# Attention with a conditioned query and key on one core: step 29 keeps its exponentials, six loads change their queue, two first blocks are loaded as halves

## The chip, the core and the metric

The kernel runs on one core of a Trainium2 chip. A core has five engines that run beside each other, each with its own queue of instructions in a fixed order: TensorE (PE in the profile; PEld is its loading of weights) for matrix products, VectorE (DVE), ScalarE (ACT), GpSimd (POOL) and SyncE (SP), which here only issues DMAs. ScalarE and GpSimd issue DMAs too. An engine that waits for a semaphore holds everything behind it in its queue. PE writes its results to PSUM, eight banks of 128 partitions by 512 floats; VectorE and ScalarE read them there.

The metric is the time of one execution in microseconds on the device. Lower is better.

## What is computed

`x` is (8, 512, 512), `cond` (8, 512), the three weights (512, 512), all float32. There are 16 heads of 32 columns.

```python
Q = split_heads(x @ Wq.T + bq);  K = split_heads(x @ Wk.T + bk);  V = split_heads(x @ Wv.T + bv)
cQ = Q + split_heads(tokens @ Wq.T + bq)     # tokens = cond[:, None, :]
cK = K + split_heads(tokens @ Wk.T + bk)
scores = einsum('bhqd,bhkd->bhqk', cQ, cK) / sqrt(32)
out = einsum('bhqk,bhkd->bhqd', softmax(scores), V)
return x + merge_heads(out)
```

## The kernel before

**Steps.** The 8 batches and 16 heads are worked in 32 steps: step `t` is batch `t // 4` and a group `t % 4` of four heads, which fill the 128 partitions, 32 columns each. All matrices lie in SBUF; q and k of a step are held turned (`qkT`), V as rows (`vs`). The products of x with the weights are made in pairs of steps, seven quarter products in place of eight (`product`, line 451), and are spread as three items over each step of the loop (`MADE`, line 1090).

**Two ways to the exponentials.** For each step the scores are computed twice. In the *row pass* (`row_max`, line 593, and `row_scores`, 639) queries lie on the partitions: VectorE takes the row maxima, and ScalarE (`denominators`, 678) takes exponentials with the maxima as bias and adds them up, which gives the denominators. In the *crossed pass* keys lie on the partitions: the maxima, turned and split in three bfloat16 parts, are put into PSUM by a small product with ones, and the scores are added on top, so that ScalarE takes plain exponentials (`exponentials`, 742). These are multiplied by V (`times_v`, 791).

**Kept steps.** For the steps in `KEPT` (line 71), steps 1 to 28, the exponentials of the first half of the queries (`qc < KQ`, two of four blocks) are kept from the row pass in `store` (`kept[t]`, `room`). They are turned in place: VectorE turns 32x32 blocks (`turn_kept`, 656; four instructions of 128x1024 for a step), and DMAs swap the blocks across partitions (`swap_kept`, 665) in three moves of six DMAs each: aside, across, and back. The first and last move are issued by GpSimd for the most part, the rest by SyncE. Only the other half of the queries is computed crosswise (`exponentials_of_rest`, 762: two calls for a step, each of which covers two of the four key blocks), and the product with V is made by halves (`times_v_half`, 802). Step 29, 30 and 31 are not kept: `exponentials` or `crossed` (1270) computes all of their exponentials, four calls for a step.

**The loop** `thirds(t)` (1133) does, for `t` from 1 to 28: row passes of step `t + 1`, the rest of the exponentials of `t`, the weighted sum of `t - 1` with its store (`weighted`, `send`), three items of products, and the turning and swapping of step `t + 1`'s kept half.

**The order is written out by hand** for PE, ScalarE, VectorE and GpSimd (`manual_schedule`, line 235): each runs its instructions in the order of the program text. SyncE's DMAs are ordered by a scheduler, by the program text where they are ready. DMAs from SyncE and ScalarE share eight semaphores in turn, so each waits until the DMA eight places before it has landed. `TURNS`, `begin` and `released` say which PSUM banks each stage uses.

**The start** (lines 245 to 1013). Wq's first block, x's first and second block and Wk's first block are loaded, then the condition and the biases, the rest of x's first batch and of Wq (lines 245 to 264). Then SyncE issues, at line 270, sixteen loads of Wk and sixteen of Wv, each a 32-row slice in turned order, so that VectorE can finish the turn (`turn_w`, 963). PE runs products with ones while it waits (line 925), then turns blocks of Wq and x and makes the first projections. `condition` (900) multiplies the condition by the turned weights, `condition_end` (908) turns that and adds the bias, and `project_qk_end` (412) adds it to q or k. With q and k of step 0 at hand, `row_max(0, 0)` (line 988) begins the steady work. `transpose_x` (350), for the third and fourth block of x, also queues the loads of the next batch's blocks (line 363, `load_block`).

**The end** (lines 1309 to 1431). Steps 29 to 31 have no products left. `crossed` mixes the row pass of one step with the crossed pass of another; `part_of` (1023) makes a step's product with V in pieces and adds the pieces on GpSimd; `send_parts` divides and stores. For steps 30 and 31 the denominators are sums of the exponentials (`sum_of`, 1256) multiplied by ones (`times_ones`, 818). Step 31 ends with the lines 1398 to 1430; line 1431 issues the last quarter of step 30's store.

Of the kernel before, what the change touches and what calls it, by code (L numbers as in the profile page):

```python
# [17 lines left out]
def kernel(  # L18
# [38 lines left out]
    nc = tc.nc  # L57
# [13 lines left out]
    KEPT = range(1, T - 3)  # L71
# [173 lines left out]
    load_w("q", Wq, nc.sync, [0])  # L245
    load_x(0, nc.scalar)
# [19 lines left out]
    for n, w, f in (("k", Wk, HG), ("v", Wv, 0)):  # L266
        wn = ws[n].rearrange("p c (f e) -> p c f e", e=BL)
        for cc in range(NC):
            for h in range(HG):
                nc.sync.dma_start(  # L270
                    wn[h * BL : (h + 1) * BL, cc, f:], spread(w, cc * P + h * BL)[:, f:]
                )
    bvl = const.tile([P, 1], F32, tag="bvl", name="bvl")
    nc.sync.dma_start(bvl, bv.rearrange("(g p o) -> g p o", g=G, o=1)[G - 1])
    bvs = const.tile([P, G, BL], F32, tag="bvs", name="bvs")
    for h in range(HG):
        nc.sync.dma_start(
            bvs[h * BL : (h + 1) * BL],
            bv.rearrange("(o g h e) -> o h g e", o=1, g=G, h=HG)[:, h].broadcast_to([BL, G, BL]),
        )  # L280


# [382 lines left out]
    def swap_kept(t, move, last=nc.gpsimd):  # L665

        later = 6 if t % 4 == 1 else 1
# [4 lines left out]
        for n, (a, g) in enumerate(APART):  # L672
# [3 lines left out]
            (last if move == 2 or move == 0 and n >= later else nc.sync).dma_start(to, of)  # L676
# [248 lines left out]
    for _ in range(28):  # L925
        nc.tensor.matmul(warm[:, :P], onesb, onesb, start=True, stop=True)
# [26 lines left out]
    transpose_x(3, bank(3), nc.scalar.copy)  # L953
    first_part("k", pk, 0)
# [63 lines left out]
    parted = []  # L1018

# [3 lines left out]
    def part_of(t, pt, of, between=None):  # L1023

        if t in KEPT:
            for half in (1, 0):
                for kc in of:
                    times_v_half(t, kc, half, pt, of)
        else:
            for k, kc in enumerate(of):  # L1030
                if k and between:
                    between()
                times_v(t, kc, pt, of)
        if t in parts:
            p = late_part(3 + len(parted))
            parted.append(t)
            nc.scalar.copy(p, pt)
            nc.gpsimd.tensor_tensor(parts[t], parts[t], p, ALU.add)
        else:
            if not parts:  # L1040
# [422 lines left out]
```

## Time and profile before

| | |
|---|---|
| median of 3 runs | 656.83 us (656.81 to 657.03) |
| profiled execution | 658.96 us |
| its span, first to last instruction | 657.0 us |
| granted TensorE clock | 1.000 |
| DMA queue of SyncE | 232068 packets, 61.08 MB, 49.3% of 16 engines' span |
| DMA queue of GpSimd | 13104 packets, 35.80 MB, 20.4% |
| DMA queue of ScalarE | 1760 packets, 1.05 MB, 0.5% |

How to read the lines that follow in this document. A timeline row is: start, duration (both us from the start of the span), engine, line, operation, what it writes and reads, shape, number of instructions that were merged, and in brackets the idle time before it with what ended it. SPq, ACTq and POOLq rows are issues of DMAs. PE's float32 products show as two records each, and four products on 32 partitions run beside each other. A row of the chain of waits is start, duration, engine, tile and line. A row of a table by stage is the stretch, its length, and for each engine the busy time and in brackets the number of instructions, then PE's clock, the busy share of the DMA engines, and GB/s.

### The profile page before, as it was taken

To read this page: it belongs to the slowest core of one execution; us is meant where nothing else is said; L and a number is where in the kernel's file an instruction comes from. 1 tells how busy PE (TensorE), PEld (TensorE's weight loads), DVE (VectorE), ACT (ScalarE), POOL (GpSimd) and SP (SyncE) were. 2 spreads that over 40 slices of the span, in tenths; PEclk is the share of its full clock that TensorE was granted. 3 is DMA by queue.
4 is the path that set the end of the run, shared out by engine and by line. 5 is a ranking of instruction groups with operands and counts; after the bars stand their busy time and mean duration, and the time that the engine had idled before them with its cause. 6 is when DMAs were issued, how large, how long until landed. Compare 5 with 4: busy or idle time off the path is not lost.

```text
span 657.0 us, 24808 instructions
## 1 busy us (share of the span) xinstructions
PE 649.0 (99%) x9836; PEld 349.7 (53%) x9836; DVE 591.8 (90%) x823; ACT 539.4 (82%) x1372; POOL 442.8 (67%) x702
## 2 busy tenths in 40 slices
PE   9999999999999999999999999999999999999997
PEld 8345455555555555555555555555555555555432
DVE  3699999999999999999988999999999999897777
ACT  2479888889888888988887988888898888898774
POOL 3542566886767776578767777678677777767461
PEclk9999999999999999999999999999999999999999
DMA  6634587878777788878897877787889767687111
GB/s 181 105 51 66 125 167 162 174 171 187 177 158 161 150 181 180 178 160 172 187 174 162 187 159 168 169 188 162 180 192 169 158 138 165 155 176 167 27 35 32
DMA packets 247048, 99.51 MB, mean 151 GB/s; under 512 B 229130, under 2 KB 229642, under 8 KB 246932
## 3 DMA queue, kind: packets, MB, share of 16 engines
q1 hardware_dynamic: 232068, 61.08, 49.3%
q0 software_dynamic: 13104, 35.80, 20.4%
q8 instruction: 77, 1.26, 0.9%
q10 hardware_dynamic: 1760, 1.05, 0.5%
q14 instruction: 39, 0.32, 0.2%
HBM read 19.75 MB, written 8.39 MB: 43 GB/s over the span
## 4 chain that ended last, share of the span: by engine, by line
PE 92%; DMA 3%; SPq 2%; DVE 1%; issue 1%; ACT 0%; POOL 0%; DVEq 0%; ACTq 0%; POOLq 0%
PE psum L461 42%; PE psum L641 18%; PE psum L810 15%; PE psum L779 7%; PE psum L768 3%; PE psum L794 2%; DMA store<-store 2%; SPq L270 1%; PE psum L750 1%; PE psum L404 1%; DMA store<-in_L_cond_Wk_dram 1%; PE psum L1287 1%; PE psum L820 1%; PE psum L747 0%; DVE nmax L650 0%
## 5 line engine op out<-in xcount | busy, mean ns | idle before, releaser
L695 ACT ACTIVATE psum<-psum,nmax 128x512 f32<-128x512 f32 x255 | 169.4, 669 | 4.8 <-DVE nmax L589 3.9
L676 POOL DMA_DIRECT2D store<-store x273 | 136.1, 503 | 42.0 <-DMA store<-store 27.1
L695 ACT ACTIVATE store<-psum,nmax 128x512 f32<-128x512 f32 x197 | 135.3, 701 | 34.7 <-DVE nmax L589 25.3
L589 DVE TENSOR_REDUCE nmax<-psum 128x1 f32<-128x512 f32 x220 | 141.3, 679 | 20.5 <-PE psum L641 18.3
L650 DVE TENSOR_REDUCE nmax<-psum 128x2 f32<-128x1024 f32 x126 | 152.7, 1213 | 1.3 <-PE psum L641 1.3
L641 PE MATMUL psum<-kT,qT 32*128 32x512 f32 x1024 | 145.1, 616 | 0.0
L789 ACT ACTIVATE store<-psum 128x512 f32<-128x512 f32 x224 | 115.7, 602 | 23.4 <-PE psum L779 23.4
L660 DVE STREAM_TRANSPOSE store<-store 128x1024 f32<-128x1024 f32 x112 | 134.2, 1218 | 0.0
L810 PE MATMUL psum<-store,v 128*32 128x256 f32 x1792 | 103.1, 381 | 1.3 <-issue 1.3
L810 PEld LDWEIGHTS psum<-store,v 128*32 128x32 f32 x1792 | 55.2, 110 | 57.5 <-ACT wT_q L628 20.5
L641 PEld LDWEIGHTS psum<-kT,qT 32*128 32x128 f32 x1024 | 56.6, 183 | 35.9 <-issue 21.1
L883 POOL TENSOR_TENSOR res<-res,recs 128x512 f32<-128x512 f32 x30 | 31.4, 1047 | 60.2 <-DVE res L882 60.0
L779 PE MATMUL psum<-qT,kT 32*128 32x256 f32 x896 | 57.9, 373 | 0.0
L695 ACT ACTIVATION_READ_ACCUMULATOR psum<-psum,nmax 128x1 f32 x255 | 54.2, 213 | 0.0
L461 PE MATMUL psum<-wc_v,xc 128*32 128x256 f32 x768 | 47.7, 379 | 0.0
L204 POOL TENSOR_TENSOR xr<-xr,bvs 128x512 f32<-128x512 f32 x30 | 38.5, 1282 | 11.2 <-DMA x<-in_x_dram 11.1
L779 PEld LDWEIGHTS psum<-qT,kT 32*128 32x128 f32 x896 | 43.9, 184 | 3.5
L461 PE MATMUL psum<-xc,wc_q 128*32 128x256 f32 x720 | 44.6, 379 | 0.0
L461 PE MATMUL psum<-xc,wc_k 128*32 128x256 f32 x720 | 44.5, 379 | 0.0
L695 ACT ACTIVATION_READ_ACCUMULATOR store<-psum,nmax 128x1 f32 x197 | 42.5, 216 | 0.0
L884 POOL TENSOR_TENSOR res<-res,xr 128x512 f32<-128x512 f32 x30 | 38.4, 1279 | 2.4
L461 PE MATMUL psum<-xT,wT_k 128*32 128x256 f32 x480 | 34.5, 382 | 0.0
(193 smaller groups left out, 1027.1 us busy)
## 6 DMA issues: line engine op xcount, KB each, us to landing
store<-store POOLq DMA_DIRECT2D x273, 128.0 KB, 3.6
store<-store SPq DMA_DIRECT2D x231, 128.0 KB, 2.4
out_dram<-res SPq DMA_DIRECT2D x122, 64.0 KB, 3.4
xr<-in_x_dram SPq DMA_DIRECT2D x120, 64.0 KB, 2.7
x<-in_x_dram SPq DMA_DIRECT2D x112, 64.0 KB, 3.0
w_q<-in_L_cond_Wq_dram SPq DMA_DIRECT2D x4, 256.0 KB, 4.1
w_v<-in_L_cond_Wv_dram SPq DMA_DIRECT2D x16, 64.0 KB, 2.5
w_k<-in_L_cond_Wk_dram SPq DMA_DIRECT2D x16, 48.0 KB, 2.9
```

The costliest lines, as they stand in the source:

```text
L204: nc.gpsimd.tensor_tensor(xr[t], xr[t], bias, ALU.add)
L461: nc.tensor.matmul(pt[r], still[:, r], moving, start=(kc == kcs[0]), stop=(kc == kcs[-1]))
L589: nc.vector.tensor_reduce(nmax[t][:, qc, j : j + 1, 0], pt, AX.X, ALU.max, negate=True)
L641: nc.tensor.matmul(pt, qkT["q", t][r, qc * P : (qc + 1) * P], qkT["k", t][r, :], start=True, stop=True,)
L650: nc.vector.tensor_reduce(nmax[t][:, qc, pr * 2 : pr * 2 + 2, 0], pt, AX.X, ALU.max, negate=True)
L660: nc.vector.transpose(e, e)
L676: (last if move == 2 or move == 0 and n >= later else nc.sync).dma_start(to, of)
L695: nc.scalar.activation(to, of, AF.Exp, bias=nmax[t][:, qc, j, :], accum_out=sums[t][:, qc, j, :],)
L779: nc.tensor.matmul(bank[j][:, i * HS : (i + 1) * HS], qkT["k", t][r, kc * P : (kc + 1) * P], qkT["q", t][r, rest], start=False, stop=(i == 1),
L789: nc.scalar.activation(e[:, i, :], bank[pr * 2 + i], AF.Exp)
L810: nc.tensor.matmul(pt[j * HD : (j + 1) * HD, half * HS : (half + 1) * HS], vs[b % 2][:, kc, (g * HG + j) * HD : (g * HG + j + 1) * HD], e, ...
L884: nc.gpsimd.tensor_tensor(y, y, xr.pop(t), ALU.add)
```

## The change

`KEPT` takes in step 29, so steps 1 to 29 are kept. The loop still runs for steps 1 to 28. In step 28 VectorE turns step 29's kept half, two pieces after the first item and two after the second (`TURNED_LAST`), its maxima are turned by a DMA as in the other steps, and its swaps are issued after the second item, three of the first move and three of the last by SyncE. In the other steps SyncE issues two of the first six moves where it issued one (all six in every fourth step, as before).

Step 29 is written anew: two row passes of step 30, the two halves of step 28's product with V around the first `exponentials_of_rest(29)`, a row pass of step 30, the second `exponentials_of_rest(29)`, half of step 29's product around a row pass of step 31 and the turning of step 30's maxima, which is behind `split_max` on VectorE. The second half of step 29's product follows in step 30. The pieces are no longer added on GpSimd, since each half is complete.

In the last steps GpSimd makes two of the sums of exponentials that VectorE made (`sum_of(t, acc, 2)` and `3`, second pair). ScalarE copies the last denominators out of PSUM and VectorE then multiplies the copy; they are turned ahead of the last block. The last quarter of step 30's store moves from ScalarE's last instruction to SyncE.

At the start the first block of Wq and of x are each loaded as two halves of 64 rows, one from SyncE and one from ScalarE. Of Wk's sixteen loads SyncE issues ten; ScalarE issues six, behind its copy for the fourth block of x. Wv's loads and `bv` stand behind these in the text, so also behind the loads that `transpose_x` queues. Four of 28 products with ones go. `condition("k")` moves straight behind `condition("q")`.

```diff
-    KEPT = range(1, T - 3)
+    KEPT = range(1, T - 2)
...
-    load_w("q", Wq, nc.sync, [0])
-    load_x(0, nc.scalar)
+    xs[0] = early[:, 3, :]
+    for to, of in ((ws["q"][:, 0, :], Wq[:P, :]), (xs[0], x[0, :P, :])):
+        nc.sync.dma_start(to[: P // 2], of[: P // 2])
+        nc.scalar.dma_start(to[P // 2 :], of[P // 2 :])
     load_x(1)
...
-    for n, w, f in (("k", Wk, HG), ("v", Wv, 0)):
+    def load_spread(n, w, f, ccs, queue=nc.sync, hs=range(HG)):
         wn = ws[n].rearrange("p c (f e) -> p c f e", e=BL)
-        for cc in range(NC):
-            for h in range(HG):
-                nc.sync.dma_start(
+        for cc in ccs:
+            for h in hs:
+                queue.dma_start(
                     wn[h * BL : (h + 1) * BL, cc, f:], spread(w, cc * P + h * BL)[:, f:]
                 )
...
+    load_spread("k", Wk, HG, (0, 1))
+    load_spread("k", Wk, HG, (2,), nc.sync, (0, 1))
...
-        later = 6 if t % 4 == 1 else 1
+        later = 3 if t == KEPT[-1] else 6 if t % 4 == 1 else 2
...
-            (last if move == 2 or move == 0 and n >= later else nc.sync).dma_start(to, of)
+            here = n >= later if t == KEPT[-1] else move == 2 or move == 0 and n >= later
+            (last if here and move != 1 else nc.sync).dma_start(to, of)
...
-    for _ in range(28):
+    for _ in range(24):
...
     transpose_x(2, bank(0))
     transpose_x(3, bank(3), nc.scalar.copy)
+    load_spread("k", Wk, HG, (2,), nc.scalar, (2, 3))
+    load_spread("k", Wk, HG, (3,), nc.scalar)
+    load_spread("v", Wv, 0, range(NC))
...
     condition("q", bank(6))
+    condition("k", bank(5))
     project_qk_part(1, "q", 0, bank(7))
     condition_end("q", bank(1), nc.vector)
     project_qk_end(0, "q", pq)
-    condition("k", bank(5))
...
+    TURNED_LAST = {(0, 2): 2, (1, 2): 2}
...
-    for t in KEPT:
+    for t in KEPT[:-1]:
         thirds(t, iter(MADE[(t - 1) % G * 3 :]))
...
     t = T - 3
-    row(4)
-    exponentials(t, 0)
-    row_max(t + 1, 1)
+    begin(0, HG)
+    first, second = row_of[0][:HG], row_of[0][HG:]
+    row_max_aside(t + 1, 1)
+    for j in range(HG):
+        row_scores(t + 1, 2, j, banks(HG + j))
+    for j in range(2):
+        nc.scalar.copy(late_part(j), banks(HG + j))
+    max_aside(t + 1, 1)
...
+    swap_kept(t, 2)
+    halves_of(t - 1, banks(0), (1,))
+    row_of[0] = [*second[:2], *first[2:], *first]
+    exponentials_of_rest(t, 0)
+    halves_of(t - 1, banks(HG), (0,))
...
+    row_max(t + 1, 3, False, HG)
+    split_max(t + 1, nc.vector)
+    exponentials_of_rest(t, 1)
+    row_of[0] = [second[0], first[3], first[1], first[0], first[2], *second[1:]]
+    halves_of(t, banks(0), (1,), (0, 1))
+    row_max(t + 2, 0, False, HG)
+    transpose_max(t + 1, banks(1), nc.scalar.copy)
+    halves_of(t, banks(0), (1,), (2, 3))
...
     t = T - 2
...
-    part_of(t - 1, banks(2), [2, 3])
+    halves_of(t - 1, banks(2), (0,))
...
-    sum_of(t, acc, 1, nc.vector, [0])
-    sum_of(t, acc, 2, nc.vector)
+    sum_of(t, acc, 2, nc.gpsimd, [1])
+    for kc in (1, 2):
+        sum_of(t, acc, kc, nc.vector, [0])
...
-    sum_of(t - 1, acc, 3, nc.vector)
+    sum_of(t - 1, acc, 3, nc.gpsimd, [1])
+    sum_of(t - 1, acc, 3, nc.vector, [0])
...
-    store_30(nc.sync, (0, 1))
+    store_30(nc.sync, (0, 1, 3))
...
-    nc.vector.tensor_tensor(part_x, pd, xr[t], ALU.mult)
...
     nc.scalar.copy(den, pd)
+    nc.vector.tensor_tensor(part_x, den, xr[t], ALU.mult)
...
-    store_30(nc.scalar, (3,))
```

More of the change, by code (lines that the diff above doesn't have):

```diff
@@ L1016, with halves_of, part_of @@
     parts = {}
-    parted = []
     def late_part(i):
         return late[0][:, i, :]
[L1023 to L1040, printed above, removed]
-                parts["all"] = stage.tile([P, NC, D], F32, tag="w", name="parts")
-            parts[t] = parts["all"][:, t % NC, :]
-            nc.scalar.copy(parts[t], pt)
+    def halves_of(t, pt, halves, among=range(NS)):
+        for half in halves:
+            for kc in among:
+                times_v_half(t, kc, half, pt)
+    def part_of(t, pt, of):
+        for kc in of:
+            times_v(t, kc, pt, of)
+        parts[t] = stage.tile([P, NC, D], F32, tag="w", name="parts")[:, 0, :]
+        nc.scalar.copy(parts[t], pt)
     def denominators_of(t, pd):
@@ L1181, in thirds @@
             load_blocks()
+            if t + 1 in KEPT and i == (2 if t + 1 < KEPT[-1] else 1):
+                moves = range(2)
+            else:
+                moves = []
             if i == 2:
@@ L1337 @@
         bias_residual(u)
-    part_of(t - 1, banks(2), [2, 3])
+    halves_of(t - 1, banks(2), (0,))
+    nc.scalar.copy(whole[t - 1][:, :HS], banks(2)[:, :HS])
     spread_sums(apart, banks(1))
@@ L1345 @@
     part_of(t, banks(2), [0])
-    send_parts(t - 1, den)
+    send_sums(t - 1, whole[t - 1], den)
     row(2)
```

78 lines of the change are left out of this document (35 added, 43 removed).

## The prediction

> **What bounds the kernel now.** I read the page first, then the chain of waits in order of time, then the timeline of the start and of the end, where the change works.
>
> ```profile
> PE 649.0 (99%) x9836; PEld 349.7 (53%) x9836; DVE 591.8 (90%) x823; ACT 539.4 (82%) x1372; POOL 442.8 (67%) x702
> ...
> PE 92%; DMA 3%; SPq 2%; DVE 1%; issue 1%; ACT 0%; POOL 0%; DVEq 0%; ACTq 0%; POOLq 0%
> ...
> L660 DVE STREAM_TRANSPOSE store<-store 128x1024 f32<-128x1024 f32 x112 | 134.2, 1218 | 0.0
> ```
>
> TensorE (PE) is busy in 99% of the span and holds 92% of the chain. Removed PE work should shorten the run, unless a wait takes its place. Two stretches are not simply PE. The first is the start:
>
> ```profile
> 8.99 1.87 SPq L270
> ...
> 16.95 2.23 DMA w_k<-in_L_cond_Wk_dram
> ...
> 19.31 0.59 DVE wT_k L965
> ...
> 19.94 1.04 PE psum L904 x2
> ...
> 24.20 1.07 PE psum L641 x8
> ```
>
> Here the chain lies on SyncE's issues of Wk (L270), then on the last transfer, on VectorE's last turn of Wk, and on `condition("k")` (L904). At 24.20 the steady work begins with `row_max(0, 0)`. From there to the end of the loop the steps are even but for one place:
>
> ```profile
> 337.48 2.08 PE L641 MATMUL psum<-kT,qT 32*128 32x512 f32 x16
> ```
> ```profile
> 377.97 2.01 PE psum L641 x16
> ...
> 416.52 2.01 PE psum L641 x16
> ```
>
> These L641 rows open every second step. 377.97 to 416.52 is 38.55 us, 337.48 to 377.97 is 40.49: a stall of 1.94 us in all. The profiled execution took 658.96 us (span 657.0), the median is 656.83, 2.13 less; I take this stall to be that execution's own. The sum below is a difference, made in its clock and applied to both: 658.96 for a profile that stalls again, 656.83 for the runs. The forecast is of the runs.
>
> **The start, part by part.** Sixteen loads of Wk left SyncE one behind the other; now SyncE issues ten and ScalarE six.
>
> ```profile
> 1.06 3.17 PE L926 MATMUL psum<-onesb 128*128 128x128 bf16 x28 [1.06 <-DVE onesb L259]
> ...
> 6.46 10.97 SPq L270 DMA_DIRECT2D w_k<-in_L_cond_Wk_dram  x16
> ...
> 9.91 0.59 ACT L361 COPY xT<-psum 128x512 f32<-128x512 f32 x1 [3.29 <-PE psum L358]
> ...
> 14.24 0.60 ACT L322 ACTIVATE wT_q<-psum 128x512 f32<-128x512 f32 x1 [3.75 <-PE psum L313]
> ...
> 15.28 1.03 DVE L965 STREAM_TRANSPOSE wT_k<-w_k 128x384 f32<-128x384 f32 x2
> ...
> 16.30 1.06 PE L904 MATMUL psum<-wT_q,condT 128*32 128x512 f32 x8
> ```
>
> An issue of SyncE takes 0.53 us where nothing holds it (16 of Wv in 8.47, below). Without its last six SyncE's part ends near 14.3 (6.46 + 10.97 - 6 x 0.53) and lands 2.23 later, by 16.5. ScalarE can issue from 10.50, the end of its copy at 9.91, and is idle until 14.24. Six issues take 3.2 us; with one stall like the 1.87 row 4.5: they end at 15.0 and land near 17.2. The copy at 14.24 then runs at 15.0, ahead of 16.30, where PE first needs it. VectorE has turned the first two blocks by 16.3 and turns the other two by about 17.7 instead of 19.9. `condition("k")`, now placed straight behind `condition("q")`, ends near 18.5. Behind it PE has the 3.2 us that lie today between 20.98 (the end of L904) and 24.20, and the 1.1 that stood between the two conditions (a projection at the pace of L404, and four transposes): it reaches `row_max(0, 0)` at 22.8 instead of 24.20, 1.4 us earlier.
>
> Not all of it stays, since the loads of Wv come later.
>
> ```profile
> 17.47 8.47 SPq L270 DMA_DIRECT2D w_v<-in_L_cond_Wv_dram  x16
> ...
> 28.41 4.15 SPq L173 DMA_DIRECT2D x<-in_x_dram  x8
> ```
> ```profile
> 27.62 1.89 DVE L965 STREAM_TRANSPOSE wT_v<-w_v 128x512 f32<-128x512 f32 x3
> ```
>
> `transpose_x(2)` and `transpose_x(3)` queue eight loads of x's next blocks on SyncE (L363). They were written behind Wv and now stand ahead of it. So Wv starts at 14.3 + 4.2 = 18.5 (before 17.47) and ends 8.5 later, at 27.0, landing at about 29.2 by the 2.23 of the Wk row. VectorE takes its instructions in order: the last of the three turns, which begin at 27.62 today and take 0.63 each, can't run before 29.2. The row maxima queued behind it then start near 29.9, no sooner than today, while PE is 1.4 ahead; ScalarE's exponentials wait for them, and PE waits for the bank that these free. PE has some slack in its banks, so I put the loss at 0.5 and keep 0.9 us. Bounds: 1.4 if Wv costs nothing, and -0.6 if the first turn of Wv is held too and the 1.0 by which Wv is later comes on top of the whole 1.0 that VectorE is behind (1.4 - 2.0).
>
> The halves of Wq and x add two issues, one on SyncE and one on ScalarE, of 0.40 us (row below), and four of 28 warming products go (4 x 0.113 = 0.45). The loads behind them (the second block of x, Wk's first block, the biases) are issued later by as much. Whatever is won or lost here, up to 0.45 each way, PE spends waiting for Wk near 17.3. I take 0, with 0.2 for the range.
>
> ```profile
> 0.74 0.40 SPq L231 DMA_DIRECT2D w_q<-in_L_cond_Wq_dram  x1
> ```
>
> [...]
>
> **The loop.** In three of four steps SyncE takes one more of the first six moves and GpSimd one fewer, about 0.5 us each way. PE, at 99%, shows no wait for these moves, so 0, with 0.3 either way.
>
> **Step 29 kept.** Half of its exponentials now come from the row pass.
>
> ```profile
> 598.09 0.39 PE L768 MATMUL psum<-maxT,onesb 3*128 3x512 bf16 x4
> ...
> 599.18 1.19 PE L641 MATMUL psum<-kT,qT 32*128 32x512 f32 x8
> ...
> 607.49 0.40 PE L731 MATMUL psum<-identb,split 128*128 128x128 bf16 x4
> 607.82 1.07 PE L461 MATMUL psum<-wT_v,xT 128*32 128x256 f32 x16
> ...
> 609.68 0.39 PE L747 MATMUL psum<-maxT,onesb 3*128 3x512 bf16 x4
> ...
> 610.77 1.02 PE L641 MATMUL psum<-kT,qT 32*128 32x512 f32 x8
> ```
> ```profile
> 609.68:624.37 14.69, 14.69 (x177) 6.83 (x173) 11.11 (x15) 10.49 (x21) 6.07 (x9) 1.00 0.02 4
> ```
>
> One `exponentials` takes 1.09 us (609.68 to 610.77), one `exponentials_of_rest` as much (598.09 to 599.18) and covers two blocks. Step 29 has four of the first and will have two of the second: 2.18 less. The window up to step 30 is 14.69 us. Written out at PE's spacings it will hold four row passes at about 0.97, products with V of 3.7 and 1.9, two of 1.09, transposes 0.33 and sums 0.2: 12.1, so 2.6 less, the extra 0.4 from the crossed order that goes. The transposes of step 29's maxima leave PE in step 28 (0.33, 607.49 to 607.82), since the maxima now go by DMA. Together 2.9.
>
> What hides the added work: VectorE turns four more 128x1024 blocks in step 28 (4 x 1.22 = 4.9 us); the two gaps it has there are these:
>
> ```profile
> 600.23 1.29 DVE L589 TENSOR_REDUCE nmax<-psum 128x1 f32<-128x512 f32 x2 [2.99 <-PE psum L641]
> ...
> 605.68 1.29 DVE L589 TENSOR_REDUCE nmax<-psum 128x1 f32<-128x512 f32 x2 [1.27 <-PE psum L641]
> ```
>
> The first pair fits into 2.99; the second pair is 1.1 late, which only delays step 30's first maxima, in banks that PE takes again after 609. In step 29 PE will wait once: the transposes of step 30's maxima come about 4.0 us behind the start of its last row pass (0.97, 1.09, half a product with V 0.93, 0.97). In step 31 the same chain took 4.9 us (row pass at 631.54, transposes at 636.42), a crossed one. I charge 0.7 and keep 2.2. Bounds: 2.9, and 0.5 if the swaps are late too (below).
>
> ```profile
> 631.54 0.70 PE L641 MATMUL psum<-kT,qT 32*128 32x512 f32 x2
> ...
> 636.42 0.40 PE L731 MATMUL psum<-identb,split 128*128 128x128 bf16 x4 [0.33 <-DVE split L712]
> ```
>
> **The end.** Two sums of 1.18 us leave VectorE for GpSimd, where one takes 2.36 (same as L1259 there).
>
> ```profile
> 645.93 2.36 DVE L1261 TENSOR_TENSOR acc<-acc,store 128x1024 f32<-128x1024 f32 x2
> ```
> ```profile
> 646.57 2.07 ACT L760 ACTIVATE store<-psum 128x512 f32<-128x512 f32 x4 [0.99 <-PE psum L750]
> ...
> 653.83 0.48 ACTq L1388 DMA_DIRECT2D out_dram<-res  x1
> ```
> ```profile
> 647.29 1.67 PE L820 MATMUL psum<-acc,ones 128*32 128x512 f32 x6
> ```
>
> VectorE's last sum ends at 648.29 and holds PE's L820; 2.36 us earlier, ScalarE's last exponential at 648.64 is the later one, and PE finishes 0.65 sooner. The last store was issued by ScalarE at 653.83; it moves to SyncE ahead of the last block's, whose data come about 0.9 sooner. I take 1.2 for the whole end (bounds 0, if ScalarE holds everything anyway, and 1.4).
>
> Sum: 0.9 + 2.2 + 1.2 = 4.3 us. 656.83 - 4.3 = 652.5 (a profile that stalls: 654.7).
>
> **Rivals.**
> 1. *Wv holds VectorE*: the start's bound of -0.6 in place of +0.9. For it: 27.62 is served with hardly a wait today. Against: PE's banks give some slack. 656.83 - 2.8 = 654.0.
> 2. *The swaps of step 29 are late*, and PE waits in step 30 for the kept half.
>
> ```profile
> 285.54 8.55 SPq L676 DMA_DIRECT2D store<-store  x7
> ```
> ```profile
> store<-store POOLq DMA_DIRECT2D x273, 128.0 KB, 3.6
> ```
> ```profile
> 297.80 0.49 POOL L676 DMA_DIRECT2D store<-store  x1 [1.02 <-DMA store<-store]
> ```
>
> In a step of the loop the moves last from 285.54 to 297.80, and 3.6 more to land: 16 us. Begun at 606.8, when the turns are done, they would land at 622.8; PE needs them near 623. Against it: SyncE has no other loads then. Late by 1.7: 654.2.
> 3. *GpSimd and VectorE slow each other* in the last sums, which no row shows side by side. If they serialize, 4.7 us of GpSimd's take VectorE's 2.36 back and 1.2 more: 652.5 + 2.4 = 654.9.
> 4. *Slower: ScalarE is held by its six issues.* They stand in its queue ahead of the copy at 14.24, which feeds `condition("q")`. SyncE's own issues of Wk took 1.87 where the queue was full; six of these take 11.2 us from 10.50, the copy ends at 22.3, `condition("q")` starts 6 us late, `row_max(0, 0)` at 28.8 instead of 24.20: 4.6 lost, 3.4 won: 658.0. It decides from 1.67 us an issue (the copy then ends at 21.1, and 3.4 is lost). Against it: SyncE's 16 took 10.97 in all, 0.69 each.
> 5. *The change doesn't do what it says*: the three late edits hide behind other waits, and only the two saved exponentials less the wait of 0.7 show: 656.83 - 1.5 = 655.3.
>
> **How the numbers follow.** Forecast 0.50, rival 1 0.13, 2 0.10, 3 0.05, 5 0.07, 4 0.15 (in its weaker forms no change). Own range of the forecast: 650.9 (1.4 + 2.9 + 1.4 and 0.2 of the head) to 653.6 (start 0.4, step 29 1.8, end 1.0). The range of 8 in 10 leaves out rival 4 and a little below: 650.9 to 655.6. 0.2 us is about what a measurement tells from no change. Faster 0.85, same 0.03, slower 0.12, the last two both out of rival 4's share.
>
> **What would show it.** Start: the last Wk turn near 17.1 instead of 19.31, and L641's first pass near 22.8; a gap on VectorE ahead of the last Wv turn shows rival 1, six long issues on ScalarE rival 4. Step 29: two rest rows, no L731 in step 28, step 30's first pass 2.5 us earlier than 624.37 relative to the loop's end; a wait of L810 for a DMA in step 30 shows rival 2. End: L820 not held by VectorE; sums longer than 1.18 and 2.36 show rival 3. The forecast is wrong at its root if PE's busy time falls by 3 us and the span does not.

## The result and the profile after

| | before | after |
|---|---|---|
| median | 657.35 us (9 runs beside the changed kernel) | 662.44 us (9 runs, 661.27 to 664.92) |
| ratio to before, 95% interval | | 1.0072 (1.0047 to 1.0096) |
| profiled execution, its span | 658.96, 657.0 us | 662.44, 660.7 us |
| granted TensorE clock | 1.000 | 0.994 |

The change makes the kernel slower by 0.7%, some 4.7 us, where 4.3 us less were forecast. The page of the profile after: busy time by engine, and the chain of waits by engine.

```profile
PE 647.6 (98%) x9852; PEld 350.5 (53%) x9852; DVE 597.1 (90%) x829; ACT 534.4 (81%) x1364; POOL 435.1 (66%) x682
...
PE 94%; DMA 2%; DVE 1%; issue 0%; SPq 0%; ACT 0%; DVEq 0%; POOL 0%; POOLq 0%
```

PE is busy for 1.4 us less than the 649.0 of before, in a span that is 3.7 us longer: work went away, and waits came. The 657.0 of before hold the stall of 1.94 that the prediction set aside, so without it the profiles are 5.64 us apart. The waits stand in three places. The first is the start; its chain of waits:

```profile
2.26 6.07 DMA store<-in_x_dram
...
20.15 1.97 PE psum L901 x16
...
26.62 1.07 PE psum L637 x8
```

The chain now runs over a load of x and then over PE without a break, no longer over Wk. Both conditions (L901) follow each other at once, as the change meant it, but they begin at 20.15 (20.08 in the timeline), where `condition("q")` began at 16.30 in the timeline; the first row pass stands at 26.62 instead of 24.20 (26.55 and 24.13 in the timeline, which the experiments below go by). Stretches of the start before (busy time of PE, PEld, DVE, ACT, POOL, then clock, busy share of the DMA engines, GB/s), and then after:

```profile
3.00:4.00 1.00, 1.00 (x12) 0.95 (x9) 0.00 (x0) 0.64 (x2) 0.00 (x0) 1.00 1.06 404
4.00:5.00 1.00, 0.92 (x8) 0.73 (x6) 0.00 (x0) 0.00 (x0) 0.00 (x0) 1.00 1.06 408
```
```profile
3.00:4.00 1.00, 0.80 (x8) 0.53 (x5) 0.00 (x0) 0.90 (x1) 0.00 (x0) 1.00 1.09 172
4.00:5.00 1.00, 0.63 (x4) 0.42 (x4) 0.00 (x0) 0.83 (x3) 0.00 (x0) 1.00 1.07 125
...
3.90:7.30 3.40, 0.67 (x5) 0.49 (x6) 0.00 (x0) 1.28 (x3) 0.00 (x0) 1.00 0.93 230
7.30:10.70 3.40, 3.35 (x16) 2.62 (x16) 1.01 (x2) 0.59 (x1) 0.00 (x0) 0.50 0.94 301
```

The DMA engines count as just as busy, yet move 172 and 125 GB/s where they moved 404 and 408. PE, busy for 0.67 us of the 3.40 from 3.9 to 7.3, then gets a clock of 0.50 for 3.4 us. The load at 2.26 in the chain is not one of the halves: it is the second block of x, a whole load issued behind them, and it lands at 8.33.

From the first row pass to step 29 both kernels go alike: 24.20 to 609.68 before, less the stall of 1.94 and the 0.33 of the transposes that left step 28, is 583.21; after it is 26.62 to 609.89, 583.27. The other two places lie behind that. PE's timeline after, from step 29 on, with the idle time in brackets:

```profile
609.89 2.08 PE L637 MATMUL psum<-kT,qT 32*128 32x512 f32 x16
...
622.92 0.70 PE L637 MATMUL psum<-kT,qT 32*128 32x512 f32 x2
...
626.85 1.93 PE L807 MATMUL psum<-store,v 128*32 128x256 f32 x32 [1.72 <-ACT store L1292]
628.57 0.26 PE L842 MATMUL psum<-apart,modulo 128*32 128x16 f32 x8
...
638.84 0.60 PE L728 MATMUL psum<-identb,split 128*128 128x128 bf16 x4 [2.56 <-DVE split L709]
639.38 1.94 PE L791 MATMUL psum<-store,v 128*32 128x512 f32 x8
```

Step 29 took 13.03 us (609.89 to 622.92) in place of 14.69. At 626.85 PE waits 1.72 us with the product of the kept half, and at 638.84 it waits 2.56 us for the split maxima of step 31 and then runs at half speed: the granted clock is 0.50 from 638.75 to 642.16, and L791 takes 1.94 instead of 1.07. The bracket at 626.85 names a group of activations that was done at 626.28. It is not what PE waits for: without the swaps (e4_noswap below) PE goes on at 625.01, while that group runs to 626.24. What is late is the swapping, in SyncE's and GpSimd's timeline:

```profile
611.40 11.28 SPq L673 DMA_DIRECT2D store<-store  x12
```
```profile
620.88 1.71 POOL L673 DMA_DIRECT2D store<-store  x3 [7.60 <-DMA store<-store]
...
635.89 2.35 POOL L1251 TENSOR_TENSOR acc<-acc,store 128x1024 f32<-128x1024 f32 x1
```

The last is issued at 622.7 (611.40 + 11.28), and PE goes on at 626.85. The last row is the sum that went to GpSimd. Beside it, VectorE:

```profile
634.25 1.21 DVE L646 TENSOR_REDUCE nmax<-psum 128x2 f32<-128x1024 f32 x1
635.50 0.49 DVE L706 CAST split<-nmax 128x16 bf16<-128x16 f32 x1
636.03 2.25 DVE L707 TENSOR_TENSOR rest<-nmax,split 128x16 f32<-128x16 f32 x1
638.32 0.20 DVE L708 CAST split<-rest 128x16 bf16<-128x16 f32 x1
```

A subtraction of 128x16 takes 2.25 us and ends when GpSimd's sum does (635.89 + 2.35 = 638.24). Three suspects, then: the halves, the late swaps, the sums on GpSimd.

### The profile page after: what moved, and what is told of

It reads as the page before. It is cut to its first block, busy times and chain, and to the rows that moved or that the text cites. A ratio compares the mean times of both kernels' runs of the same rounds, so it can differ in the third digit from the quotient of the medians.

```text
span 660.7 us, 24918 instructions
## 1 busy us (share of the span) xinstructions
PE 647.6 (98%) x9852; PEld 350.5 (53%) x9852; DVE 597.1 (90%) x829; ACT 534.4 (81%) x1364; POOL 435.1 (66%) x682
## 3 DMA queue, kind: packets, MB, share of 16 engines
q10 hardware_dynamic: 3648, 1.28, 0.9%
q8 instruction: 78, 1.28, 0.8%
## 4 chain that ended last, share of the span: by engine, by line
PE 94%; DMA 2%; DVE 1%; issue 0%; SPq 0%; ACT 0%; DVEq 0%; POOL 0%; POOLq 0%
PE psum L457 43%; PE psum L637 18%; PE psum L807 15%; PE psum L776 7%; PE psum L765 3%; PE psum L400 2%; PE psum L791 2%; DMA store<-store 1%; PE psum L747 1%; DMA store<-in_x_dram 1%; PE psum L744 0%; PE psum L817 0%; DVE rest L707 0%; PE psum L309 0%; PE psum L354 0%
## 5 line engine op out<-in xcount | busy, mean ns | idle before, releaser
L673 POOL DMA_DIRECT2D store<-store x258 | 128.7, 503 | 64.1 <-DMA store<-store 50.2
L692 ACT ACTIVATE store<-psum,nmax 128x512 f32<-128x512 f32 x204 | 140.0, 701 | 35.7 <-DVE nmax L585 25.9
L692 ACT ACTIVATE psum<-psum,nmax 128x512 f32<-128x512 f32 x248 | 164.7, 669 | 3.4 <-DVE nmax L585 2.6
L585 DVE TENSOR_REDUCE nmax<-psum 128x1 f32<-128x512 f32 x225 | 144.3, 678 | 18.1 <-PE psum L637 16.0
L646 DVE TENSOR_REDUCE nmax<-psum 128x2 f32<-128x1024 f32 x125 | 151.3, 1211 | 0.0
L637 PE MATMUL psum<-kT,qT 32*128 32x512 f32 x1024 | 142.2, 617 | 0.0
L786 ACT ACTIVATE store<-psum 128x512 f32<-128x512 f32 x232 | 119.8, 603 | 27.0 <-PE psum L776 27.0
L656 DVE STREAM_TRANSPOSE store<-store 128x1024 f32<-128x1024 f32 x116 | 138.8, 1216 | 0.0
L807 PE MATMUL psum<-store,v 128*32 128x256 f32 x1856 | 106.8, 381 | 1.7 <-ACT store L1292 1.7
L807 PEld LDWEIGHTS psum<-store,v 128*32 128x32 f32 x1856 | 57.2, 110 | 58.7 <-ACT wT_q L624 21.2
L776 PE MATMUL psum<-qT,kT 32*128 32x256 f32 x928 | 59.9, 373 | 0.0
```

Source lines behind the costliest of these rows:

```text
L585: nc.vector.tensor_reduce(nmax[t][:, qc, j : j + 1, 0], pt, AX.X, ALU.max, negate=True)
L637: nc.tensor.matmul(pt, qkT["q", t][r, qc * P : (qc + 1) * P], qkT["k", t][r, :], start=True, stop=True,)
L646: nc.vector.tensor_reduce(nmax[t][:, qc, pr * 2 : pr * 2 + 2, 0], pt, AX.X, ALU.max, negate=True)
L656: nc.vector.transpose(e, e)
L673: (last if here and move != 1 else nc.sync).dma_start(to, of)
L692: nc.scalar.activation(to, of, AF.Exp, bias=nmax[t][:, qc, j, :], accum_out=sums[t][:, qc, j, :],)
```

## The experiments

Ratios are to the kernel before, on the same chip, with 95% intervals; 0.001 is 0.66 us.

**Whole first blocks again** (e1_whole): the changed kernel with

```diff
-    for to, of in ((ws["q"][:, 0, :], Wq[:P, :]), (xs[0], x[0, :P, :])):
-        nc.sync.dma_start(to[: P // 2], of[: P // 2])
-        nc.scalar.dma_start(to[P // 2 :], of[P // 2 :])
+    load_w("q", Wq, nc.sync, [0])
+    load_x(0, nc.scalar)
```

> The changed kernel, with the first blocks of Wq and of x loaded whole again (one DMA each, Wq from SyncE, x from ScalarE); everything else as changed. Theory (the halves make the start late): x's first block lands near 4.4 us instead of 7.1, condition(q) starts near 16.3 instead of 20.08, the first row pass stands at 22.5 to 23.0 instead of 26.55, the time is 3.5 to 3.9 us below the changed kernel's (about 1.0 us above the kernel before). Rival (ScalarE's six loads of Wk, or condition(k) behind condition(q), make it late): the first row pass stays above 26, the time changes by less than 0.5 us.

Median 658.81, ratio 0.9997 (0.9962 to 1.0033) against 1.0072: 4.9 us won back, with wide intervals (0.9 to 8.8 from end to end); the spans of the two profiles differ by 4.2. Stretches, then PE and VectorE in the timeline:

```profile
3.00:4.00 1.00, 0.80 (x8) 0.53 (x5) 0.00 (x0) 0.65 (x2) 0.00 (x0) 1.00 1.05 395
4.00:5.00 1.00, 0.82 (x8) 0.85 (x8) 0.00 (x0) 0.16 (x1) 0.00 (x0) 1.00 1.07 410
```
```profile
22.66 1.14 PE L635 MATMUL psum<-kT,qT 32*128 32x512 f32 x8
...
28.73 0.71 DVE L971 STREAM_TRANSPOSE wT_v<-w_v 128x512 f32<-128x512 f32 x1 [1.28 <-DMA w_v<-in_L_cond_Wv_dram]
```

The DMA engines are back at 400 GB/s and the first pass stands at 22.66, where the theory had it. VectorE does wait 1.28 us for Wv, but that holds nobody: the row pass that stood at 62.94 before stands at 61.46, so the whole 1.47 by which the first pass is ahead of the profile of before (24.13) is still there.

**The halves alone** (e2_halves, and again as e17_rows), and **halves of columns** (e16_columns): the kernel before with the four lines above in the other direction; for columns the slices are `[:, : D // 2]` and `[:, D // 2 :]`, from the same two queues.

> The kernel before, with the first blocks of Wq and of x each loaded as two halves from SyncE and ScalarE; nothing else changed. Theory (the halves alone make the start late): the first loads land 2 to 3.5 us later, the first row pass stands at 26.5 to 28 instead of 24.13, the time is 2.4 to 3.8 us above before. Rival (the halves cost only their two issues, at most 0.45 us, as the prediction had it): the first row pass within 0.5 of 24.13, the time within 0.5 us of before.

> The kernel before with halves of 64 rows once more, to stand beside the halves of columns on one chip. Theory: 130 to 280 GB/s between 3 and 5 us, 1.5 to 3.5 us above before.

> The kernel before, with the first blocks of Wq and of x each loaded as two halves from SyncE and ScalarE, but halves of 256 columns over all 128 rows, not of 64 rows. [...] Rival (two queues at once on one block, or four DMAs in place of two, are slow): below 280 GB/s between 3 and 5 us, as with the halves of rows, and the time 1.5 to 3.5 us above before.

Rows: 1.0039 (1.0006 to 1.0072) and 1.0058 (1.0039 to 1.0076), 2.6 and 3.8 us slower, with the first row pass at 27.90 and 26.56. Columns: 1.0019 (1.0005 to 1.0033), 1.2 slower. Stretches of e17_rows, then of e16_columns, and a row of PE in the latter:

```profile
3.00:4.00 1.00, 1.00 (x12) 1.00 (x10) 0.00 (x0) 0.90 (x1) 0.00 (x0) 1.00 0.83 184
4.00:5.00 1.00, 1.00 (x7) 0.68 (x4) 0.00 (x0) 0.58 (x2) 0.00 (x0) 1.00 0.97 170
```
```profile
3.00:4.00 1.00, 1.00 (x12) 1.00 (x10) 0.00 (x0) 0.99 (x2) 0.00 (x0) 1.00 0.96 332
4.00:5.00 1.00, 1.00 (x10) 1.00 (x8) 0.00 (x0) 0.18 (x2) 0.00 (x0) 1.00 0.81 305
```
```profile
7.58 0.78 PE L360 MATMUL psum<-ident,store 128*128 128x128 f32 x4 [2.25 <-DMA store<-in_x_dram]
```

With the same queues and the same number of DMAs, 128 rows move 332 and 305 GB/s and 64 rows 184 and 170; why, no run shows. By the ratios most of the loss is in the 64 rows (3.8 against 1.2 us on one chip, and the intervals do not meet); the interval of the columns is 0.3 to 2.2 us. The profiles do not show that difference. With columns the first block of x was there for PE at 4.72, but the second, a whole load issued behind, only at 7.58; the first row pass stood at 26.49, where rows have 26.56, and the spans are 657.8 and 657.9. The execution in that profile took 659.57, and four more of the twelve took 659.5 or longer; the other seven took 656.2 to 658.8. So a split of either kind can delay the load behind it (8.33 in the changed kernel, 7.58 here), and the columns seem to escape in some executions; why that load is late, no run shows. With rows the loss varies too: in six profiles with halves of rows from two queues and 24 or 28 products with ones the first pass stood between 24.41 (e5_swap, below) and 27.90, in four of the start of before between 23.26 and 24.13.

**Each block's halves from one queue** (e7_onequeue):

> The changed kernel with both halves of Wq's first block issued by SyncE and both halves of x's by ScalarE; the same four DMAs of 64 rows, each block from one queue. Theory (DMAs of 64 rows are slow, from whichever queue): the DMA engines again move less than 200 GB/s between 3 and 5 us, x's second half lands after 6.5, the first row pass stays above 25.5. Rival (two queues that write one block are what is slow): 300 GB/s and more between 3 and 5 us, x's second half lands by 5.2, the first row pass stands below 24.

One execution, 667.16 us; 277, 186 and 221 GB/s in the stretches from 3 to 6. x's second half landed at about 4.5, not after 6.5 as the theory had it, but the second block of x only at 7.9, and the first row pass stood at 27.77. So this run fits neither in full: the slow rate stays without two queues on one block, the late half of x itself does not. What is late here is what was late with columns, the whole load behind. Part of the 27.77 is PE's pace: its first projection (L400, eight records) took 3.60 us in place of 1.99.

**PE kept busy** (e6_warm): the changed kernel with `range(52)` for `range(24)` at the products with ones.

> The changed kernel with 52 products with ones in place of 24 at the start, so that PE works on until 6.9 us while the halves of x land. Theory (of the 3.8 us by which condition(q) is late about 1.5 are PE at half its clock, which follows its idle time from 4.7 to 7.26): no granted clock of 0.5 near 7 to 11 us, the eight turns at L352 take 1.1 us and not 2.23, the first row pass stands at 24.7 to 25.4 instead of 26.55. Rival (the clock does not follow PE's idle time, all 3.8 us are late loads): the clock is 0.5 there again or the first row pass stays above 26.2.

One execution, 660.95 us. Stretch and timeline:

```profile
6.90:10.30 3.40, 3.40 (x26) 2.89 (x24) 1.62 (x5) 1.18 (x2) 0.00 (x0) 1.00 0.84 271
```
```profile
7.20 1.21 PE L354 MATMUL psum<-ident,store 128*128 128x128 f32 x8
...
24.89 1.14 PE L637 MATMUL psum<-kT,qT 32*128 32x512 f32 x8
```

The loads come about as late as in the changed kernel, but the clock stays at 1.00, and the first pass stands at 24.89 instead of 26.55: in these single profiles, of the 3.9 us by which 26.55 is behind the whole blocks, 1.7 are clock and about 2.2 are loads. How much of PE's pace is lost differs between executions: with 24 products and whole blocks the first pass stood at 22.66 in one profile and at 24.81 in another (e8_best, below), where PE's first products took up to twice their time until about 9.6.

**The sums back on VectorE** (e3_sums), in the changed kernel, and **on GpSimd alone** (e12_gpsums), in the kernel before:

```diff
-    sum_of(t, acc, 2, nc.gpsimd, [1])
-    for kc in (1, 2):
-        sum_of(t, acc, kc, nc.vector, [0])
+    sum_of(t, acc, 1, nc.vector, [0])
+    sum_of(t, acc, 2, nc.vector)
...
-    sum_of(t - 1, acc, 3, nc.gpsimd, [1])
-    sum_of(t - 1, acc, 3, nc.vector, [0])
+    sum_of(t - 1, acc, 3, nc.vector)
```

> The changed kernel, with the two sums of exponentials that went to GpSimd back on VectorE. Theory (GpSimd's add holds VectorE's small subtraction `rest` in split_max, PE waits for it and then runs at half clock): rest takes about 0.2 us instead of 2.25, PE's wait ahead of the transposes of step 31's maxima falls from 2.56 to below 0.6, no half clock behind it, and the time is 2 to 3.3 us below the changed kernel's. Rival (the maxima of step 31 come late because the row pass before them does): the wait stays above 2 us, the time within 0.5 us of the changed kernel's, or above it since VectorE has 2.36 us more to do.

> The kernel before, with the two sums of exponentials on GpSimd that the change moved there, nothing else. Theory (GpSimd's add holds VectorE's subtraction of split_max): rest takes about 2 us instead of 0.2, PE waits 2 us and more ahead of the transposes of step 31's maxima and then runs 3.41 us at half clock; VectorE's last sum is 1 us sooner; in all the time is 1.5 to 2.5 us above before. Rival (the prediction's: the sums on GpSimd free VectorE): 0.4 to 0.7 us below before.

Back: 1.0047 (1.0021 to 1.0073), 1.6 us better than the changed kernel by the ratios, 2.9 by the spans of the profiles (657.8 and 660.7); the two intervals overlap, so the runs do not settle whether it is the 2 to 3.3 expected. Alone: 1.0043 (1.0031 to 1.0055), 2.8 us worse than before. Timeline of e3_sums, of e12_gpsums on VectorE, GpSimd and PE, and its stretches:

```profile
635.58 0.18 DVE L707 TENSOR_TENSOR rest<-nmax,split 128x16 f32<-128x16 f32 x1
...
636.33 0.40 PE L728 MATMUL psum<-identb,split 128*128 128x128 bf16 x4 [0.51 <-DVE split L709]
```
```profile
633.86 2.35 POOL L1261 TENSOR_TENSOR acc<-acc,store 128x1024 f32<-128x1024 f32 x1
633.99 2.25 DVE L710 TENSOR_TENSOR rest<-nmax,split 128x16 f32<-128x16 f32 x1
636.69 2.36 POOL L1261 TENSOR_TENSOR acc<-acc,store 128x1024 f32<-128x1024 f32 x1 [0.48 <-ACT store L760]
636.80 0.40 PE L731 MATMUL psum<-identb,split 128*128 128x128 bf16 x4 [2.40 <-DVE split L712]
637.64 2.48 DVE L1259 TENSOR_TENSOR acc<-store 128x1024 f32<-128x1024 f32 x1
```
```profile
635.20:638.60 3.40, 1.80 (x20) 0.80 (x24) 2.77 (x5) 1.34 (x3) 2.92 (x2) 0.99 0.36 61
638.60:642.00 3.40, 3.40 (x20) 0.34 (x16) 2.75 (x2) 1.87 (x4) 0.45 (x1) 0.50 0.00 0
```

0.18 us without GpSimd's sum, 2.25 with it, in a kernel that has nothing else of the change. VectorE's next sum, at 637.64, is held in the same way: it takes 2.48 where L1259 took 1.22 before, and ends 1.07 behind GpSimd's second (640.12 against 639.05), as if it only began there. So a sum of 2.35 us on GpSimd held VectorE for 2.07 us (2.25 less 0.18), to save it 1.18. Not everything is held: in the changed kernel the maxima read from PSUM (L646 at 631.12) took 1.21 beside GpSimd's sum of 631.22 to 633.58, the mean of all 125 being 1.21, and the turning of one tile (L879 at 632.41) took 0.65 beside the same sum, as in 28 others of its line (median 0.65).

**No swaps of step 29** (e4_noswap): `swap_kept` returns at once for step 29.

> The changed kernel without the eighteen DMAs that swap step 29's kept half (this leaves out part of the turning of step 29's first half of queries). Theory (these DMAs come late and PE waits 1.72 us for the last of them in step 30): the wait ahead of the product with V of the kept half is gone, the second crossed pass of step 30 starts 1.7 to 1.8 us earlier, the time is 1.5 to 1.8 us below the changed kernel's. Rival (PE runs on to the next wait, ahead of the transposes of step 31's maxima, whose end GpSimd's sum sets): that wait grows from 2.56 to above 4 us, and the time changes by less than 0.5 us.

```profile
625.01 1.93 PE L809 MATMUL psum<-store,v 128*32 128x256 f32 x32
...
637.01 0.40 PE L730 MATMUL psum<-identb,split 128*128 128x128 bf16 x4 [2.57 <-DVE split L711]
```

The wait is gone, and the next one did not grow (2.57 against 2.56), so the rival falls; the span was 658.7, 2.0 shorter. The median, 662.01 with 1.0060 (1.0028 to 1.0092), does not tell that from the changed kernel: the size of the gain rests on the one profile.

**Swaps earlier, first try** (e5_swap). Step 29's blocks are set aside in `store[:, 6:8]`, GpSimd takes half of each move, and the residual loads go to GpSimd:

```diff
+            room_aside = store[:, 6:8] if t == KEPT[-1] else between
-            (last if here and move != 1 else nc.sync).dma_start(to, of)
+            (last if here else nc.sync).dma_start(to, of)
...
-                load_residual(t + 1)
+                load_residual(t + 1, nc.sync if t + 1 < KEPT[-1] else nc.gpsimd)
```

> The changed kernel, with step 29's swaps begun earlier: they are set aside in another part of the store, so that they need not wait for step 28's last move; GpSimd takes half of each of the three moves; the loads of the residuals of steps 29 and 30 go from SyncE to GpSimd, behind the swaps. Theory (PE waits 1.72 us in step 30 because these DMAs begin at 611.4 and not at 606.8): the first of them is issued by 610.2, the wait ahead of the kept half's product is below 0.3 us, the second crossed pass of step 30 stands 5.9 us (not 5.8 from a first pass 1.7 later) behind, that is 4.0 to 4.3 us, behind the first, and the time is 1.5 to 1.8 us below the changed kernel's. Rival (the swaps are bound by their own three landings, not by their begin): the wait stays above 1 us. Rival (GpSimd, with eleven more issues, becomes late for the sums and stores of the end): the wait goes, the time falls by less than 0.7 us.

1.0082 (1.0056 to 1.0109): no gain. In its profile the wait for step 31's maxima (2.57 again) was followed by products at about half their pace until 643.30 (L792 and L748 took 1.92 to 1.94 in place of 1.06 and 1.03), 6.5 us behind the end of the wait, where in the changed kernel L791 is back at 1.07 after 4.0. GpSimd's timeline and PE's:

```profile
616.36 2.58 POOL L191 DMA_DIRECT2D store<-in_x_dram  x4
618.96 0.32 POOL L833 TENSOR_TENSOR apart<-sums,which 128x64 f32<-128x64 f32 x1
619.24 1.52 POOL L674 DMA_DIRECT2D store<-store  x3
```
```profile
624.79 1.93 PE L808 MATMUL psum<-store,v 128*32 128x256 f32 x32 [1.77 <-DMA store<-store]
```

SyncE's first move was issued at 608.14, 0.36 us behind the begin of step 29 (607.78 here), where it had been 1.51 behind (611.40 and 609.89). The swaps still ended late, by the edit's own doing: the loads of step 30's residual (L191) stood in GpSimd's queue ahead of the last moves.

**The good parts together, first try** (e8_best): whole blocks, these swaps, the end of before.

> The changed kernel with whole first blocks, step 29's swaps begun earlier (as in the run that moves them alone), and the end as it was before: all sums of exponentials on VectorE, the last store's quarter on ScalarE behind the last block, the last denominators multiplied straight out of PSUM. What stays of the change: Wk over two queues with condition(k) behind condition(q), and step 29 kept. Theory (these two parts are worth what the first passes show, 1.47 and 1.66 + 0.33 us, when the waits that the rest added are gone): first row pass at 22.7, span 651.6 to 652.6, the time 2.3 to 3.4 us below the kernel before, 653.4 to 654.6. Rival (the end takes back what step 29 gains, since VectorE's maxima of step 31 and its sums set it): the wait ahead of the transposes of step 31's maxima is above 1 us, the time no more than 1.5 us below the kernel before.

1.0000 (0.9985 to 1.0014): no better than before. PE waited 1.62 us for the swaps, for the reason just shown, and in the profiled execution the first pass stood at 24.81, with PE idle for 0.67 us behind its 24 products with ones and slow until about 9.6 (L352 took 1.91 where e1_whole has 1.12). That slowness is read from the products' times; the clock column of that stretch shows 1.00, so that it was the clock is inferred.

**Both mended** (e9_two), **step 29 alone** (e10_keep, and again e15_keep2), **Wk alone** (e11_wk, with 28 products e13_wk28), **both with 28 products** (e14_two28):

```diff
+    swap_kept(t, 2)
+    load_residual(t + 1, nc.gpsimd)
     aparts[t] = masked(t)
-    swap_kept(t, 2)
...
-    for _ in range(24):
+    for _ in range(30):
```

> As the run that combined whole first blocks, earlier swaps and the end of before, with two things mended: GpSimd issues the residual loads of step 30 behind the last swaps, not ahead of them, and 30 products with ones warm PE up instead of 24. Theory (step 29 kept and Wk over two queues are worth 1.99 and 1.47 us where no wait is added): first row pass at 22.6 to 23.0 with the full clock from the first 5 us on, PE's wait ahead of the kept half's product in step 30 below 0.3 us, span 651.8 to 653.0, the time 2.0 to 3.2 us below the kernel before. Rival (the swaps are bound by their three landings): that wait stays above 1 us, the time is within 1.6 us of before. Rival (the gain goes into the waits for step 31's maxima): PE's wait there is above 1.5 us.

> The same with the start as it was before: all of Wk from SyncE, Wv behind it, condition(k) where it was, 28 products with ones. What stays of the change is step 29 kept, with its swaps earlier. Theory: first row pass at 24.1 to 24.4, the time 1.6 to 2.2 us below the kernel before. Rival (step 29's gain is taken back by the end): within 0.7 us of before.

> The kernel before, with Wk over two queues, Wv behind it, condition(k) straight behind condition(q), and 30 products with ones. Theory: first row pass at 22.6 to 23.0, and all of the 1.47 us by which that is earlier stays to the end: the time is 1.2 to 1.6 us below before. Rival (Wv, later by 1 us, takes 0.5 back, as the prediction had it): 0.7 to 1.1 us below. Rival (ScalarE's issues lengthen the loads): no gain.

> The kernel before, with Wk over two queues, Wv behind it and condition(k) straight behind condition(q), now with the 28 products with ones of before. Theory (the start's 1.4 us came from one execution, in which SyncE's issues of Wk stood 1.1 us longer than in other executions, so the edit is worth nothing as a rule): the first row pass stands 6.9 to 7.2 us behind condition(q), no sooner than the 6.7 of the start of before where Wk comes in time, and the time is within 0.5 us of before. Rival (the edit gains 0.9, as it seems on top of step 29): 0.7 to 1.1 us below before. Rival (the edit costs 1.3, as it seemed alone): 1.0 to 1.6 us above before.

> Step 29 kept with earlier swaps, whole first blocks, the end of before, Wk over two queues, and 28 products with ones in place of 30. Theory: within 0.5 us of the same kernel with the start of before. Rival (the edit gains 0.9): 0.7 to 1.1 below it. Rival (the edit costs 1.3): 1.0 to 1.6 above it.

> Step 29 kept with earlier swaps on the start of before, once more, as what the other is compared with. Theory: 1.6 to 2.2 us below the kernel before, as in the first run of it.

| kernel | median | ratio to before, 95% |
|---|---|---|
| e9_two (step 29, Wk, 30 products) | 654.12 | 0.9957 (0.9944 to 0.9970) |
| e14_two28 (step 29, Wk, 28 products) | 655.14 | 0.9973 (0.9962 to 0.9984) |
| e10_keep (step 29) | 654.99 | 0.9968 (0.9956 to 0.9981) |
| e15_keep2 (the same again) | 655.17 | 0.9972 (0.9961 to 0.9983) |
| e11_wk (Wk, 30 products) | 658.20 | 1.0035 (1.0009 to 1.0061) |
| e13_wk28 (Wk, 28 products) | 657.69 | 1.0013 (1.0002 to 1.0024) |

Step 29 kept is worth 1.8 to 2.1 us; it beats both kernels. In e9_two the product that waited begins without a wait; its moves are issued by 617.7 on SyncE and by 617.05 on GpSimd, 10.7 and 10.1 us behind the begin of step 29 (606.99) instead of 12.8:

```profile
607.37 10.36 SPq L672 DMA_DIRECT2D store<-store  x9
```
```profile
622.24 1.93 PE L806 MATMUL psum<-store,v 128*32 128x256 f32 x32
```

Wk over two queues shows no gain: 655.14 against 655.17 on one chip with the same products, and slower alone. (With 30 products it was 654.12 against 654.99 on another chip, where the intervals overlap.) Timeline of e10_keep on SyncE, then on PE, and of e14_two28 on PE:

```profile
6.32 9.76 SPq L270 DMA_DIRECT2D w_k<-in_L_cond_Wk_dram  x16
```
```profile
16.65 1.07 PE L905 MATMUL psum<-wT_q,condT 128*32 128x512 f32 x8
...
23.35 1.14 PE L640 MATMUL psum<-kT,qT 32*128 32x512 f32 x8
```
```profile
16.09 1.07 PE L900 MATMUL psum<-wT_q,condT 128*32 128x512 f32 x8
16.98 1.84 PE L900 MATMUL psum<-wT_k,condT 128*32 128x512 f32 x8
...
23.26 1.14 PE L635 MATMUL psum<-kT,qT 32*128 32x512 f32 x8
```

All sixteen issues by SyncE took 9.76 us here, 9.85 and 10.33 in two other profiles of that start, and 10.97 only in the one I predicted from. Then PE goes from `condition("q")` to the first row pass in 6.70 us (7.83 in the one I predicted from), and with Wk over two queues in 7.17, since `condition("k")`, now placed earlier, waits itself (1.84 instead of 1.07). Why the edit costs 0.9 to 2.3 us where it stands alone stays open: the profile of e11_wk shows the transposes of step 31's maxima at 633.91, no later than before (636.42, with the stall of 1.94 ahead). Its last issue of a store stands 2.17 earlier (651.66 and 653.83), yet the span ends only 0.6 earlier (656.4 and 657.0): 1.6 us lie behind the last issue of a store.

## Why the prediction was wrong

- **Start, 0.9 gained: the term was nothing.** The steps came as described: six issues of ScalarE in 3.62 us, four turns of Wk in a row, both conditions together. But about 1.1 of the 1.4 were in that one execution alone: from `condition("q")` to the first row pass PE took 7.83 us there, with the 1.87 row among SyncE's issues, where three other profiles of the same start took 6.69 to 6.84. I had taken a stall of 1.94 in the loop as that execution's own, and built on this one. The 0.5 charged for Wv was wrong too (in e1_whole it holds nobody), so rival 1 falls; so does rival 4, ScalarE was not held; that SyncE's queue was full at the 1.87 row, no run shows.
- **Halves, 0 with 0.2: failed**, the first of the two steps that turn the sign. They cost 2.6 to 3.8 us. I priced the issues only, and argued that a loss would vanish in PE's wait for Wk near 17.3. The transfers themselves came late, the second block of x at 8.33 among them; PE's work between x's first blocks and `condition("q")` has no gap, so every late load moved it whole, and the idle PE lost clock besides (0.50 from 7.29 to 10.70).
- **Loop, 0: right** (583.21 and 583.27).
- **Step 29, 2.2: right in size, 1.99 in the trace and about 1.9 in the runs, once the swaps are early.** As changed, rival 2 takes 1.7 of it back. Its estimate put the begin at 606.8, when the turns would be done; they were done at 607.36, but SyncE's queue held stores, residual loads and the transposition of the maxima ahead, and step 28's last move still used the set-aside space: 611.40.
- **End, 1.2: failed**, the second step that turns the sign. The two sums cost 2.8 alone. Rival 3 had the mechanism (they serialize) but not its place: not sum against sum at the very end, but the small subtraction in `split_max(31)` (2.25 us in place of 0.18), for which PE waits, and the half clock behind it. My sum for the end was weak by its own rows, too: VectorE's last sum ended at 648.29, ahead of ScalarE's last exponential at 648.64, so a faster VectorE could win little there. The other edits of the end were not tried one by one and show no gain together: from the last products with V to the end of the span it is 7.8 us before (649.24 to 657.0) and after (652.89 to 660.7), and 8.7 in e3_sums.

Added up, halves (2.6 to 3.8), sums (2.8), late swaps (1.7) and step 29 (-1.9) make 5.2 to 6.4 against the 4.7 measured; those that come from ratios have intervals 1.4 us wide or wider, so the sum need not meet. By stage, the two profiles give: 2.42 later at the first row pass, 0.06 in the loop, 1.99 won at step 29, 3.87 lost from there to the transposes of step 31's maxima (15.92 us, before 12.05: the late swaps and the held subtraction), and 1.28 behind them, where the clock was halved; together the 5.64.

## What to carry to other kernels

Price a split load by when its parts and the loads behind it land, not by its issues; of the two splits tried, the one that kept all 128 partitions in each part cost less by the ratios (1.2 against 3.8 us), but not nothing. Before work goes from VectorE to GpSimd, list VectorE's small two-input operations beside it (here a subtraction of 128x16, 2.25 us in place of 0.18) and who waits for them. A term that rests on one stall of one profile needs a second profile, and a move of DMAs to another queue is worth only what stands ahead of them there allows (PE waited 1.77 us for the swaps behind four loads on GpSimd in e5_swap, and not at all with the loads behind them in e9_two).

## What the runs showed of the hardware

- PE's granted clock falls to 0.50 for 3.41 us at a time: from 7.29 to 10.70 and from 638.75 to 642.16 in the changed kernel, and once more at 659.23, where the span ends 1.43 us later. In e5_swap most products from 636.79 to 643.30 took nearly twice their time: two such steps in a row, by an estimate from these rows. A step at half clock costs a busy PE 1.7 us, an estimate: half of the 3.41. The falls of the changed kernel begin 631.46 and 20.48 us apart, 185 and 6 times 3.4133, with 3.413 measured for each of the two whole steps, so in this execution the steps seem to keep one grid. Waits of 2.56 (changed kernel) and 2.40 (e12_gpsums) were each followed by one; the 1.72 at 626.85 was not.
- A DMA of 64 rows took 0.56 to 0.82 us to issue, one of 128 rows by 256 columns, with as many bytes, 0.40 to 0.44. That the rows are the reason is not shown: the whole blocks issued right behind the 64 rows took 0.60 to 0.62 too, where before they took 0.42 and 0.46.
